# A graph layer with indirect gathers: shorter pauses behind them, an earlier table, and messages in fours across row blocks

## The chip, the cores and the metric

The kernel runs on one core of one Trainium2 chip. The metric is the device time of one execution in microseconds; the profile is of one such execution, and its span runs from the first to the last instruction.

## What is computed

There are N = 2708 nodes with D = 128 features and a dense, mostly zero adjacency matrix `adj` (N x N, rows normalised, with a diagonal). Two layers, each with a residual and a layer norm:

```python
# layer 0: a hyperbolic graph convolution
XW = mobius_matvec(W, X)
gamma = 2.0 / max(1.0 - sum(XW * XW), EPS)
two_mean = (A @ (gamma * XW)) / clamp_abs(A @ (gamma - 1.0))
m = mobius_scalar_mul(0.5, two_mean)
AXW = mobius_scalar_mul(A.sum(-1), m)
x = layernorm(x + expmap0(relu(logmap0(AXW))))
# layer 1: messages over the edges
s = x @ msg_w[:, :D].T ; d = x @ msg_w[:, D:].T
messages = gelu(s[:, None, :] + d[None, :, :] + msg_b)
aggregated = einsum('ijd,ij->id', messages, adj)
h = gelu(concat([x, aggregated]) @ upd_w.T + upd_b) + x
x = layernorm(x + layernorm(h) * ln_w + ln_b)
```

Layer 1 is only worked out for the edges where `adj` isn't zero. All norms of a row (`_norm`, tanh, artanh) are scalars per node.

## The kernel before, in words

The nodes are 22 row blocks of 128. The host only lays the inputs out anew; the kernel does the rest.

**Setup.** `x @ W` and the scalars of every node give `y`, the right side of the first layer's product.

**Layer 0**, a loop over the row blocks. `layer0(b)` loads the block's transposed adjacency `aT` (1408 KB, two buffers), takes its sign on ScalarE (`sgn`, L323) and multiplies by `y` with 22 fp32 products on TensorE (L328). From the signs, `keys` builds numbers that tell where the non-zero columns are (bf16 products, L354, and the eight largest by VectorE, L362), and `extract` turns them into lists of edges in tiles of 128: `J` (column), `rid` (row), `R` (a 0/1 matrix from edge to row), and `F`, the address of the edge's value in `adj` (L452, three buffers). Then GpSimd gathers the values `V` with one indirect DMA per tile of 128 edges. There are 25 lists and 99 tiles (the table `TILES`); `LATE` says how many tiles of a list are reserved for the column blocks from `SPLIT` = 16 on. A block's two steps of `extract` run during the next two blocks.

**Gathers.** All indirect DMAs go through one helper, which puts a pause behind each: a tiny GpSimd instruction of which nothing uses the result.

```python
def gather(o, src, at):
    last = nc.gpsimd.indirect_dma_start(...)
    with tc.issue_after(last.ins):
        nc.gpsimd.tensor_tensor(gap, ones[:, :1], nhalf, op=OP.pow)
```

`issue_after` only orders the pause behind its gather; the scheduler may place it later. The gathers are at L193, the pauses at L197.

**The epilogue of layer 0**, `layer0_end(b0, b1)`, runs on chunks of row blocks, `CHUNKS = [(0, 16), (16, 22)]`: the hyperbolic scalars (L468 to L497, short VectorE instructions on columns of 6 or 16), ReLU and layer norm (L508 to L521), then a transpose (L524), the two products of layer 1 (L532), `s_nm` in SBUF and `dt`, which is written to the DRAM `table` (L539). The first chunk is spread over the blocks after 16, the second comes at the end with high priority.

**Messages.** For each row block, `messages` takes its tiles in fours at most: gather the rows of `table` into `dd` (a ring of 7 buffers of four), spread `s_nm` to the edges with `R` (L690), add (L695), Gelu (L696), and sum to the rows with a matrix `rv` made from the values (L692, L698). `own` adds the node's own edge. For the first 8 row blocks (`EARLY`) the tiles below the split are done first, all after the last epilogue in the program; part of them is gathered into an `aT` buffer. A block's sum then goes through `node`: copy (L660), update product (L609 to L612), Gelu (L613), and in groups of blocks (`GROUPS`) two layer norms (`first`, `finish`, scratch pool `fin` with two buffers) and the output. `step()` advances every waiting `node` by one stage after each call's four.

**Fallback.** At the end flags are summed; if the lists couldn't hold all edges, a dense loop would run. It does not with these inputs.

Each engine executes its instructions in the order of the program as the scheduler has laid it out; the scheduler goes by priorities and by its own estimates of time.

Of the kernel before, what the change touches and what calls it, by code (L numbers as in the profile page):

```python
# [10 lines left out]
F32 = mybir.dt.float32  # L11
U32 = mybir.dt.uint32
# [14 lines left out]
CHUNKS = [(0, 16), (16, 22)]  # L27
GROUPS = [(0, 8), (8, 6), (14, 4), (18, 2), (20, 2)]
EARLY = 8

# [3 lines left out]
SPLIT = 16  # L34
# [3 lines left out]
def group_of(b):  # L38

    if b == 0:  # L40
        return [
            [(0, 1, 8), (1, 2, 8)],
            [(2, 4, 8), (4, 6, 4), (6, 8, 4)],
            [(8, 10, 4), (10, 12, 4), (12, 14, 4), (14, 16, 4)],
            [(16, 19, 4), (19, 22, 4)],
        ]
    s = [4, 2, 2, 1] if b == 1 else [2, 1, 1, 1] if b < 9 else [1] * 4
    return [[(0, 4, s[0]), (4, 8, s[1]), (8, 16, s[2]), (16, 22, s[3])]]
# [5 lines left out]
LATE = [0, 0, 0, 3, 2, 3, 2, 2, 1, 1, 2, 2, 2, 1, 1, 2, 1, 1, 2, 1, 2, 2, 2, 1, 1]  # L54
# [21 lines left out]
def hyperbolic_then_message_kernel(  # L76
# [64 lines left out]
    nc.gpsimd.tensor_scalar(place, place, SPAN, float(SPLIT * P), op0=OP.mult, op1=OP.add)  # L141
# [3 lines left out]
    for i in range(2):  # L145
# [4 lines left out]

    key = const.tile([P, SPLIT], I32, name="key")
    nc.gpsimd.iota(key, pattern=[[-1, SPLIT]], base=127 + 23, channel_multiplier=0)
    nc.vector.tensor_scalar(key, key, 23, None, op0=OP.logical_shift_left)
    kd = const.tile([P, SPLIT, P], BF16, name="kd")
    nc.gpsimd.affine_select(
        kd,
        key.bitcast(F32).unsqueeze(2).to_broadcast([P, SPLIT, P]),
        pattern=[[0, SPLIT], [-1, P]],
# [31 lines left out]
    gap = const.tile([P, 1], F32, name="gap")  # L190

    def gather(o, src, at):
        last = nc.gpsimd.indirect_dma_start(  # L193
            out=o, out_offset=None, in_=src, in_offset=bass.IndirectOffsetOnAxis(ap=at, axis=0)
        )
        with tc.issue_after(last.ins):
            nc.gpsimd.tensor_tensor(gap, ones[:, :1], nhalf, op=OP.pow)  # L197
# [18 lines left out]
    def cols(n):  # L216
        count[0] += 1
        return sc.tile([P, n], F32, name=f"c{count[0]}")

    def rsqrt(v, n, pool=None):  # L220

        if pool is None:
            h, t, o = cols(n).bitcast(I32), cols(n), cols(n)
        else:
            h = pool.tile([P, n], I32, name="rh")
            t = pool.tile([P, n], F32, name="rt")
            o = pool.tile([P, n], F32, name="ro")
# [41 lines left out]
    fin = ctx.enter_context(tc.tile_pool(name="fin", bufs=2))  # L269
# [46 lines left out]
    ss, ssp = cols(NB), cols(NB)  # L316

    def layer0(b):
# [3 lines left out]
        sgn = stream.tile([P, NB, P], BF16, name="sgn", bufs=1)  # L322
        nc.scalar.activation(sgn, aT, AF.Sign, accum_out=signs[:, b : b + 1])  # L323
        op = bank("mp")
        for j in range(NB):
            if j in BREAKS:
                yield
            nc.tensor.matmul(  # L328
                op[:, : D + 2], lhsT=aT[:, j, :], rhs=y[:, j, :], start=(j == 0), stop=(j == NB - 1)
            )  # L330

# [7 lines left out]
            t, v, 0.0, v, op0=OP.max, op1=OP.mult, accum_out=ssp[:, b : b + 1]  # L339
# [3 lines left out]
    def keys(l, sgn):  # L343
# [7 lines left out]
        for i, (j0, j1, _) in enumerate(groups):  # L351
            for j in range(j0, j1):
                q = j if j0 < SPLIT else j - SPLIT + 10
# [16 lines left out]
    def extract(l):  # L370
# [4 lines left out]
        def tmp(name, dt=F32, w=CMAX):  # L375
            return small.tile([P, w], dt, name=name)[:, :C]
# [50 lines left out]
        for k, s in parts:  # L427
            nc.vector.tensor_tensor_scan(scan[:, s], m[:, s], m[:, s], oe[:, l, k : k + 1], op0=OP.add, op1=OP.max)
            nc.vector.scalar_tensor_tensor(
                code[:, s], bits[:, s], 17281.0 + 768 * k, low[:, s], op0=OP.subtract, op1=OP.add  # L430
# [3 lines left out]
        F = small.tile([P, TMAX], U32, name="F", bufs=3)  # L434
# [23 lines left out]
    x1, x1T = x_sb, xT  # L458
    s_nm = mx

    def layer0_end(b0, b1):

        n = b1 - b0
        sb = slice(b0, b1)

        den, r = nom[:, sb, D], nom[:, sb, D + 1]
        di, t, v, e, f = (cols(n) for _ in range(5))
        nc.vector.tensor_scalar_max(di, den, DEN_EPS)  # L468
        nc.vector.tensor_scalar_min(t, den, -DEN_EPS)
        nc.vector.scalar_tensor_tensor(di, den, 0.0, di, op0=OP.is_ge, op1=OP.mult)  # L470
        nc.vector.scalar_tensor_tensor(t, den, 0.0, t, op0=OP.is_lt, op1=OP.mult)
        nc.vector.tensor_add(di, di, t)
        nc.vector.reciprocal(di, di)
        nc.vector.tensor_mul(v, di, di)
        nc.vector.tensor_mul(v, v, ss[:, sb])
        tn, tq = root(v, n)


        a = artanh(tn, n)
        touch(AF.Gelu, a)  # L480
        nc.vector.scalar_tensor_tensor(e, a, 0.5, r, op0=OP.mult, op1=OP.mult)
        nc.vector.tensor_scalar(e, e, FAR, -FAR, op0=OP.min, op1=OP.max)
        nc.vector.tensor_mul(e, e, tq)
        nc.vector.tensor_mul(e, e, di)

        w, p = cols(n), cols(n)
        nc.vector.tensor_sub(w, ss[:, sb], ssp[:, sb])
        nc.vector.scalar_tensor_tensor(p, e, 0.0, ssp[:, sb], op0=OP.is_ge, op1=OP.mult)
        nc.vector.tensor_scalar(t, e, 0.0, None, op0=OP.is_lt)
        nc.vector.scalar_tensor_tensor(w, w, 0.0, t, op0=OP.max, op1=OP.mult)  # L490
        nc.vector.tensor_add(w, w, p)
        nc.vector.tensor_mul(t, e, e)
        nc.vector.tensor_mul(w, w, t)
        un, uq = root(w, n)
        nc.scalar.activation(f, un, AF.Tanh)
        nc.vector.tensor_mul(f, f, uq)
        nc.vector.tensor_mul(f, f, e)  # L497
        if b1 < NB:
            touch(AF.Ln, un)

# [16 lines left out]
        for g, gn in parts:  # L517
# [9 lines left out]
            for k0 in range(0, gn, 2):  # L527
# [8 lines left out]
                last["ACT"] = nc.scalar.copy(dt[:, k0 : k0 + n2, :], sd[:, 1])  # L536
# [5 lines left out]
            last["DVE"] = nc.vector.tensor_add(nom[:, g : g + gn, :D], s_nm[:, g : g + gn, :], dt[:, :gn, :])  # L542

    last = {}
    ends, found, placed = [], [], []
    with tc.issue_after(setup.ins):
        for b in range(NB):
            work = layer0(b)
            next(work)
            for x in placed:  # L550
                next(x, None)
            placed = []
            next(work)
            for x in found:
                next(x)
            placed, found = found, []
            sgn = next(work)
            for l in of_block[b]:
                keys(l, sgn)
                found.append(extract(l))  # L560
            if b == 0 or b == NB - 1:
                for x in found:
                    next(x)
                    next(x, None)
                for x in placed:
                    next(x, None)
                found, placed = [], []
            for e in ends:
                next(e, None)
            for b0, b1 in CHUNKS:  # L570
                if b == b1 - 1 and b1 < NB:
                    ends.append(layer0_end(b0, b1))
                    next(ends[-1])
    for e in ends:
        for _ in e:
            pass
    with tc.high_priority():
        for _ in layer0_end(*CHUNKS[-1]):
            pass
# [3 lines left out]
    gd = nom  # L583
    for ins in last.values():
        ctx.enter_context(tc.issue_after(ins.ins))
    for g, n in quads:
        nc.scalar.activation(gd[:, g : g + n, :D], gd[:, g : g + n, :D], AF.Gelu)
        for k in range(n):
            nc.scalar.mul(gd[:, g + k, :D], gd[:, g + k, :D], dg[:, g + k : g + k + 1])
    xlb = y  # L590
    for g, n in quads:
        nc.vector.tensor_add(xlb[:, g : g + n, :D], x1[:, g : g + n, :], wide(rowvec["lb"], n))
# [64 lines left out]
    def node(h, k, b, b0, n, ag, more, pool):  # L657

        agT = edge.tile([P, P], F32, name="agT")
        nc.scalar.copy(agT, ag[:, :P])  # L660
# [16 lines left out]
    def ring(w):  # L677
        return edge.tile([P, 4, P], F32, name="dd", bufs=RING)[:, :w, :]

    def messages(b, ag, tiles, first, final, bins, room=ring):  # L680

        for q, k0 in enumerate(range(0, len(tiles), 4)):
            ts = tiles[k0 : k0 + 4]
            w = len(ts)
            dd = room(w)
            X = bank(bins[q % len(bins)]).rearrange("p (t d) -> p t d", d=D)[:, :w, :]
            rv = edge.tile([P, 4, P], F32, name="rv", bufs=3)
            for k, t in enumerate(ts):
                gather(dd[:, k, :], table[: SPLIT * P] if t in soon else table, J[:, t : t + 1])
                nc.tensor.matmul(X[:, k, :], lhsT=R[:, t, :], rhs=s_nm[:, b, :], start=True, stop=True)  # L690

                nc.vector.tensor_scalar(  # L692
                    rv[:, k, :], iotaN, rid[:, t : t + 1], V[:, t : t + 1], op0=OP.is_equal, op1=OP.mult
                )
            nc.vector.tensor_tensor(dd, X, dd, op=OP.add)  # L695
            nc.scalar.activation(dd, dd, AF.Gelu)  # L696
            for k in range(w):
                nc.tensor.matmul(  # L698
                    ag[:, :P],
                    lhsT=dd[:, k, :],  # L700
                    rhs=rv[:, k, :],
                    start=(first and k0 == 0 and k == 0),
                    stop=(final and k0 + k == len(tiles) - 1),
                )
            step()

    def own(b, ag):
        nc.tensor.matmul(ag[:, :P], lhsT=gd[:, b, :D], rhs=ident, start=True, stop=False)

# [7 lines left out]
    slab, quads_in = stream.tile([P, NB, P], F32, name="aT"), [0, 0]  # L717

    def roomy(w):
        quads_in[0] += 1  # L720
# [178 lines left out]
```

## Time and profile before

The time is 460.92 us, the median of three runs (460.42 to 465.71). The profiled execution took 460.36 us, its span is 458.6 us, and TensorE was granted 0.791 of its clock on average.

| engine | busy us | share of the span | instructions |
|---|---|---|---|
| TensorE, products | 327.1 | 71% | 2427 |
| TensorE, weight loads | 294.5 | 64% | 2427 |
| VectorE | 281.8 | 61% | 1517 |
| ScalarE | 198.9 | 43% | 538 |
| GpSimd | 331.3 | 72% | 495 |

No engine is busy throughout, so the shares alone don't tell what sets the end. The kernel has stages: setup to about 31 us, layer 0 to about 236, the last epilogue to about 289, messages to about 436, and the last nodes and outputs. The shares have to be read stage by stage, and the busy time of GpSimd counts the issue of a gather and the pause, not the idle time between them. The tile names of the code (`V`, `dd`, `aT`, `gap`, `F`) are the names in the profile's rows.

### The profile page before, as it was taken

Reading aid. Unit: us, or ns where it says so; the run is one execution under the profiler, and the core shown is the slowest. Engines: PE = TensorE matmul, PEld = TensorE weight load, DVE = VectorE, ACT = ScalarE, POOL = GpSimd, SP = SyncE. Lnnn points to the kernel's source line nnn. Section 1 sums busy time; section 2 is a strip of 40 time slices with the busy share of each in tenths; the row PEclk is TensorE's granted clock in tenths of the full one; section 3 lists DMA queues with packets and bytes.
Section 4 is the critical chain, followed back from the end, with each engine's and each line's share of the span. In section 5 each row is a group of like instructions: output and inputs, shape, how many; then the busy total and the mean of one; then the engine's idle time right before and its main releaser. Section 6 shows DMA issues by size and latency. Waiting matters only on the chain.

```text
span 458.6 us, 8002 instructions
## 1 busy us (share of the span) xinstructions
PE 327.1 (71%) x2427; PEld 294.5 (64%) x2427; DVE 281.8 (61%) x1517; ACT 198.9 (43%) x538; POOL 331.3 (72%) x495
## 2 busy tenths in 40 slices
PE   3359999948989999979971007693179777888820
PEld 3249999947989999977871005683168676777710
DVE  1997888832757577997765633992035434445872
ACT  2925676641747675983852303831012111124240
POOL 5400788898898898855278788998888888888200
PEclk9759999987899999998995557798556867575555
DMA  8504543523335464632501112110011111113011
GB/s 324 233 2 151 200 156 128 168 87 126 129 128 206 176 209 174 224 109 85 180 19 30 51 35 69 35 35 1 28 36 35 38 38 34 41 35 83 16 42 39
DMA packets 16238, 45.14 MB, mean 98 GB/s; under 512 B 5626, under 2 KB 11150, under 8 KB 13374
## 3 DMA queue, kind: packets, MB, share of 16 engines
q1 hardware_dynamic: 9710, 37.43, 22.6%
q0 software_dynamic: 6336, 6.55, 6.1%
q10 hardware_dynamic: 144, 0.60, 0.4%
q8 instruction: 20, 0.33, 0.3%
q14 instruction: 28, 0.23, 0.2%
HBM read 41.74 MB, written 2.83 MB: 97 GB/s over the span
## 4 chain that ended last, share of the span: by engine, by line
POOL 36%; PE 29%; DVE 15%; issue 8%; DMA 7%; ACT 3%; POOLq 0%; DVEq 0%
POOL gap L197 14%; PE mp L328 9%; POOL V L193 9%; POOL dd L193 9%; POOL aT L193 4%; DMA dd<-table_dram,J 4%; PE mp L698 4%; PE sel L442 3%; PE X L690 2%; DMA V<-in_adj_dram,F 2%; PE kx L354 2%; PE X L532 2%; PE sel L612 2%; DVE top L362 1%; DMA xT<-in_x_t_dram 1%
## 5 line engine op out<-in xcount | busy, mean ns | idle before, releaser
L193 POOL DMA_INDIRECT V<-in_adj_dram,F x99 | 99.4, 1004 | 57.4 <-DVE top L362 31.0
L328 PE MATMUL mp<-y,aT 128*128 128x130 f32 x968 | 125.8, 285 | 0.9 <-DVE y L312 0.9
L197 POOL TENSOR_TENSOR gap<-ones,nhalf 128x1 f32<-128x1 f32 x198 | 120.7, 610 | 7.1
L328 PEld LDWEIGHTS mp<-y,aT 128*128 128x128 f32 x968 | 118.0, 197 | 1.4 <-DVE y L312 1.1
L193 POOL DMA_INDIRECT dd<-table_dram,J x81 | 79.8, 985 | 25.2 <-issue 13.4
L323 ACT ACTIVATE sgn<-aT 128x2816 bf16<-128x2816 f32 x22 | 56.0, 2545 | 3.9 <-ACT junk L336 3.5
L690 PE MATMUL X<-mx,R 128*128 128x128 f32 x198 | 39.3, 343 | 25.1 <-DVE dd L695 23.5
L695 DVE TENSOR_TENSOR dd<-X,dd 128x384 f32<-128x384 f32 (+3 forms) x29 | 15.1, 526 | 63.8 <-DMA dd<-table_dram,J 60.2
L690 PEld LDWEIGHTS X<-mx,R 128*128 128x128 f32 x198 | 34.2, 250 | 27.7 <-DVE dd L695 24.6
L442 PE MATMUL sel<-z,R 128*128 128x49 f32 (+4 forms) x198 | 30.0, 288 | 22.1 <-DVE R L418 7.3
L442 PEld LDWEIGHTS sel<-z,R 128*128 128x128 f32 x198 | 26.3, 200 | 25.1 <-DVE R L418 8.3
L354 PEld LDWEIGHTS <-sgn 128*128 128x128 bf16 x484 | 29.7, 102 | 18.2 <-issue 9.6
L354 PE MATMUL kx<-kd,sgn 128*128 128x128 bf16 x484 | 35.2, 227 | 7.5 <-ACT sgn L323 7.5
L698 PE MATMUL mp<-rv,dd 128*128 128x128 f32 x116 | 29.1, 414 | 16.0 <-ACT dd L696 13.1
L696 ACT ACTIVATE dd<-dd 128x384 f32<-128x384 f32 (+3 forms) x29 | 13.9, 497 | 55.6 <-DVE dd L695 54.8
L698 PEld LDWEIGHTS mp<-rv,dd 128*128 128x128 f32 x116 | 24.5, 304 | 18.9 <-ACT dd L696 15.1
L413 ACT ACTIVATE work<-iota,mid 128x512 f32<-128x512 f32 (+3 forms) x53 | 26.8, 553 | 22.6 <-DVE mid L406 18.3
L692 DVE TENSOR_SCALAR rv<-iotaN,rid,V 128x128 f32<-128x128 f32 x99 | 30.8, 351 | 3.8 <-PE mp L698 2.9
L362 DVE MAX8 top<-kx 128x8 f32<-128x128 f32 (+3 forms) x152 | 28.5, 234 | 3.7 <-remote 1.6
L524 PE MATMUL kx<-ident,x_sb 128*128 128x128 f32 x22 | 5.8, 356 | 21.7 <-DVE x_sb L521 21.4
L452 DVE SCALAR_TENSOR_TENSOR F<-J,rid 128x3 uint32<-128x3 uint32 (+5 forms) x29 | 4.8, 165 | 26.8 <-DMA V<-in_adj_dram,F 18.7
L366 ACT ACTIVATE junk_s<-kx 128x512 bf16<-128x512 f32 (+2 forms) x25 | 14.1, 563 | 15.6 <-DVE top L362 15.4
(205 smaller groups left out, 611.5 us busy)
## 6 DMA issues: line engine op xcount, KB each, us to landing
aT<-in_adj_t_dram SPq DMA_DIRECT2D x22, 1408.0 KB
V<-in_adj_dram,F POOLq DMA_INDIRECT x99
xT<-in_x_t_dram SPq DMA_DIRECT2D x2, 704.0 KB
x_sb<-in_x_nm_dram SPq DMA_DIRECT2D x2, 704.0 KB
out_dram<-nom SPq DMA_DIRECT2D x21, 64.0 KB
dd<-table_dram,J POOLq DMA_INDIRECT x81
table_dram<-dt SPq DMA_DIRECT2D x5, 256.0 KB
pk<-in_pack_dram ACTq DMA_DIRECT2D x1, 587.5 KB
```

Source lines behind the costliest of these rows:

```text
L193: last = nc.gpsimd.indirect_dma_start(out=o, out_offset=None, in_=src, in_offset=bass.IndirectOffsetOnAxis(ap=at, axis=0))
L197: nc.gpsimd.tensor_tensor(gap, ones[:, :1], nhalf, op=OP.pow)
L323: nc.scalar.activation(sgn, aT, AF.Sign, accum_out=signs[:, b : b + 1])
L328: nc.tensor.matmul(op[:, : D + 2], lhsT=aT[:, j, :], rhs=y[:, j, :], start=(j == 0), stop=(j == NB - 1))
L354: nc.tensor.matmul(kp[:, i * P : (i + 1) * P], lhsT=sgn[:, j, :], rhs=kd[:, q, :], start=False, stop=(i == len(groups) - 1 and j == j1 - 1),)
L362: nc.vector.max(top[:, c : c + 8], seg[:, s, :])
L413: nc.scalar.activation(r0, iota[:, k0 * P : k1 * P], AF.Abs, scale=2.0, bias=mid[:, k : k + 1])
L442: nc.tensor.matmul(sp[:, k, :], lhsT=R[:, t0 + k0 + k, :], rhs=z, start=True, stop=True)
L690: nc.tensor.matmul(X[:, k, :], lhsT=R[:, t, :], rhs=s_nm[:, b, :], start=True, stop=True)
L692: nc.vector.tensor_scalar(rv[:, k, :], iotaN, rid[:, t : t + 1], V[:, t : t + 1], op0=OP.is_equal, op1=OP.mult)
L695: nc.vector.tensor_tensor(dd, X, dd, op=OP.add)
L698: nc.tensor.matmul(ag[:, :P], lhsT=dd[:, k, :], rhs=rv[:, k, :], start=(first and k0 == 0 and k == 0), stop=(final and k0 + k == len(tiles ...
```

## The change

It has these parts, in the order of the diff:

- The pause becomes the sum of two 128 x 128 tiles in place of a power of one column, and it gets high priority, so that the scheduler places it right behind its gather.
- The table is split at row block 13 in place of 16, and the lists' segments follow (`group_of`, `LATE`). `BITS` = 16 keeps the number of bit positions of the keys as before.
- The epilogue runs in three chunks. Its steps are released from within the blocks, by `PARTS`: none, one, two, two steps at successive half blocks. Its scalar part is rewritten: the two square roots go through one chain on a tile of twice the width, and the sign is carried apart.
- `F` has twelve buffers for three, `sgn` two for one, `mp` three for two, the scratch `fin` four for two; `rv` has two for three.
- The row gathers are taken out of `messages` into `fetch`. From row block 14 on (`FETCH`) a call of `fetch` follows each block, so that up to 7 fours of row gathers (the ring) stand among the value gathers of layer 0. The early messages are computed from the end of layer 0 on, between the steps of the last epilogue.
- The tiles of all row blocks form one sequence, cut into fours across the borders of blocks: 25 fours. Up to three sums are open at once. `own` is made when a block's sum opens.

Its core:

```diff
-CHUNKS = [(0, 16), (16, 22)]
+CHUNKS = [(0, 13), (13, 18), (18, 22)]
+PARTS = (0, 1, 2, 2)
+FETCH = 14
-SPLIT = 16
+SPLIT, BITS = 13, 16
...
-    gap = const.tile([P, 1], F32, name="gap")
+    gap = const.tile([P, P], F32, name="gap")
...
-        with tc.issue_after(last.ins):
-            nc.gpsimd.tensor_tensor(gap, ones[:, :1], nhalf, op=OP.pow)
+        with tc.issue_after(last.ins), tc.high_priority():
+            nc.gpsimd.tensor_add(gap, ones, ones)
...
-    fin = ctx.enter_context(tc.tile_pool(name="fin", bufs=2))
+    fin = ctx.enter_context(tc.tile_pool(name="fin", bufs=4))
...
-        sgn = stream.tile([P, NB, P], BF16, name="sgn", bufs=1)
+        sgn = stream.tile([P, NB, P], BF16, name="sgn")
...
-        op = bank("mp")
+        op = bank("mp", 3)
...
-        F = small.tile([P, TMAX], U32, name="F", bufs=3)
+        F = small.tile([P, TMAX], U32, name="F", bufs=12)
...
-        tn, tq = root(v, n)
...
-        un, uq = root(w, n)
+        a = sc.tile([P, 2, NB], F32, name="norms")[:, :, :n]
+        nc.vector.tensor_scalar_max(a, both[:, :, sb], MIN_NORM * MIN_NORM)
+        q = rsqrt(a, n, two=True)
...
+    work = fours([(b, early[b]) for b in range(EARLY)], True)
+    ahead = len(work)
+    work += fours([(b, late[b] if b < EARLY else early[b] + late[b]) for b in range(NB)], False)
...
+    def fetch():
+        if len(rooms) < (len(work) if whole else ahead):
+            dd = edge.tile([P, 4, P], F32, name="dd", bufs=RING)
+            for k, (_, t, *_) in enumerate(work[len(rooms)]):
+                gather(dd[:, k, :], table[: SPLIT * P] if t in soon else table, J[:, t : t + 1])
+            rooms.append(dd)
...
+            if b >= FETCH:
+                fetch()
...
+    for _ in layer0_end(*CHUNKS[-1]):
+        with tc.issue_after(products[-1].ins):
+            for _ in range(2):
+                messages()
```

In the order in which the scheduler lays the changed program out, GpSimd issues 77 value gathers, then 28 row gathers mixed with the value gathers of the last row blocks, then the other 71 row gathers. Nearly every gather has its pause directly behind it; five pauses stand in one row at one place.

## Prediction

> **What bounds the kernel now.** I read the chain that ended last first, then the costliest groups. GpSimd leads the chain, with the gathers and the pauses as its largest lines:
>
> ```profile
> POOL 36%; PE 29%; DVE 15%; issue 8%; DMA 7%; ACT 3%; POOLq 0%; DVEq 0%
> ...
> L193 POOL DMA_INDIRECT V<-in_adj_dram,F x99 | 99.4, 1004 | 57.4 <-DVE top L362 31.0
> ...
> L197 POOL TENSOR_TENSOR gap<-ones,nhalf 128x1 f32<-128x1 f32 x198 | 120.7, 610 | 7.1
> ...
> L193 POOL DMA_INDIRECT dd<-table_dram,J x81 | 79.8, 985 | 25.2 <-issue 13.4
> ```
>
> With the 18 row gathers into `aT` (18.8 us) GpSimd issues 198 gathers of about 1 us and 198 pauses of 0.61 us. Next, its instructions in order of time (start, us):
>
> ```profile
> 238.10 0.95 POOL L193 DMA_INDIRECT dd<-table_dram,J  x1 [0.30 <-issue]
> 239.36 0.95 POOL L193 DMA_INDIRECT dd<-table_dram,J  x1 [0.30 <-issue]
> ...
> 308.08 15.09 POOL L197 TENSOR_TENSOR gap<-ones,nhalf 128x1 f32<-128x1 f32 x24
> 323.42 1.00 POOL L193 DMA_INDIRECT dd<-table_dram,J  x1 [0.25 <-issue]
> 324.45 0.59 POOL L197 TENSOR_TENSOR gap<-ones,nhalf 128x1 f32<-128x1 f32 x1
> 325.21 0.99 POOL L193 DMA_INDIRECT dd<-table_dram,J  x1 [0.17 <-issue]
> ```
>
> A gather with its pause takes 325.21 - 323.42 = 1.79 us, one without 1.25. The first gather starts at 47.5 and the last ends at 427.1: 379.6 us, of which 198 x 1.78 = 352 are this cadence. Real holes are only about 19 us, all between 199 and 230; the largest is the wait for the table. The 24 pauses that the scheduler left behind at 236 to 272 are paid at 308 in one piece. After 427.1 there are 31.5 us of tail. The waits add one more thing:
>
> ```profile
> DVE F L452 <- DMA V<-in_adj_dram,F: 18.7, 8, 7.9
> ...
> POOL dd L193 <- DMA table_dram<-dt: 8.9, 1, 8.9
> ```
>
> `F` has three buffers, so VectorE's lists stand still until gathers have landed. The stretches show what that costs TensorE (columns: PE, PEld, DVE, ACT, POOL busy, clock, DMA share, GB/s):
>
> ```profile
> 90.00:140.00 50.00, 39.34 (x343) 36.48 (x341) 23.12 (x131) 21.74 (x53) 44.83 (x56) 0.86 0.35 122
> 140.00:190.00 50.00, 49.82 (x496) 47.45 (x496) 37.16 (x240) 35.63 (x79) 44.51 (x55) 1.00 0.56 198
> ...
> 236.00:289.00 53.00, 13.85 (x72) 9.65 (x71) 26.84 (x150) 13.63 (x41) 43.46 (x51) 0.63 0.16 44
> ...
> 340.00:390.00 50.00, 40.74 (x202) 35.97 (x202) 22.61 (x94) 10.36 (x32) 44.30 (x57) 0.70 0.15 37
> ```
>
> Layer 0 (31 to 236) is nearly TensorE's, except 90 to 140. From 236 to 289 TensorE starves behind the last epilogue while GpSimd goes on. From 289 GpSimd sets the pace again. So the end is gathers x cadence + holes + tail.
>
> **What the Trainium skill says.** "GPSIMD Engine Reference", section Elementwise, puts a two-input sum at about 2.6 cycles an element (4497 ns for 2048 fp32). No sum runs on this GpSimd, so no trace of before agrees or disagrees; I use it below. "SBUF — State Buffer", section Who interferes with whom, says that a VectorE instruction with two SBUF inputs and a GpSimd instruction that reads SBUF lock each other out. Something like it is visible: among gathers without pauses VectorE's short dependent instructions wait over a microsecond each,
>
> ```profile
> 264.14 0.18 DVE L512 BATCH_NORM_AGGREGATE mv<-st 128x2 f32<-128x6 f32 x1 [1.06 <-DVE st L511]
> 265.55 0.18 DVE L512 BATCH_NORM_AGGREGATE mv<-st 128x2 f32<-128x6 f32 x1 [1.22 <-DVE mv L512]
> ```
>
> where the trace can't say whether the reading or the writing of the gathers is at fault, but which suggests what the pauses are for: to let VectorE through. "Perfetto Trace Analysis", section DMA Instruction — SWDGE (GPSIMD), says a gather's bar ends with its descriptors, not its data; the trace agrees: a bar of 1.0 us, then waits of 2.5 to 3.4 us for `dd` in the chain.
>
> **The change, part by part.**
>
> *The pause.* 198 `pow` on 128x1 become 198 sums on 128x128, each kept behind its gather. Cadence without the pause itself: 1.78 - 0.58 (median) = 1.20 us. Lower bound of the sum: 0.30 us, the one-input tensor_scalar 128x128 at L136. Upper bound: the fixed 0.19 us of a 128x1 tensor_scalar plus 128 x 2.54 ns, the slope of the slowest elementwise row here (128x1024 in 2.79 us), 0.52; with lockouts by a busy VectorE perhaps 0.6. I take fixed 0.19 + 128 x 2.1 ns (the page's slope, an estimate) = 0.46, and add 0.02 for lockouts: cadence 1.68.
>
> *What fills the holes.* The table's first 13 blocks are written inside layer 0, so 28 row gathers (a ring of 7 fours) go in between the value gathers. In the changed program's order 77 value gathers come first, then row gathers and values in turn, 121 in all. When does the first row gather start? By count, 47.5 + 77 x 1.68 = 177. Two waits are later. SyncE holds the table's writes behind the load of block 17's `aT`, which needs block 15 done: at 176 before, minus about 14 of the stall at 90 to 140, plus the first chunk's transposes and products (13 blocks x (0.36 + 2 x 0.46) = 17 us of TensorE) = 179. Four writes through one `dt` buffer, some 2 to 3 us each, partly in flight: 187. The lists of block 14, read two blocks after its end, give 180 to 185. I take 187, so a hole of 10. Then nothing stops GpSimd: the full table is needed at the 37th row gather, 187 + 58 x 1.68 = 284, and the last epilogue should end near 262. GpSimd ends at 187 + 121 x 1.68 = 390.
>
> *F in twelve buffers, `sgn` and `mp` deeper.* Removes VectorE's 18.7 us of waiting; layer 0 ends near 224. Off the path: GpSimd is then behind. Its worth is in the 187 above.
>
> *The epilogue.* 63 short VectorE instructions per chunk become 45: 126 to 135 in all, at 0.17 us + 1.5 us, beside TensorE. The exposed last chunk has 4 blocks for 6 and saves 18 x 0.17 = 3 us. Hidden by the gathers that run on.
>
> *Fours across blocks.* 35 calls become 25, ten fewer sums and Gelus (0.53 + 0.50 us) off the path. They wait for 4 gathers, 6.7 us; TensorE per four needs about 126 us (its busy time after 236) / 25 = 5.0 us, so it keeps up. In the tail three updates instead of one follow the last four's products: 2 x 2.1 us (L609, L611, L612 at 1.83 per block, a Gelu at 0.27) = +4.2; `fin` in four buffers takes away the 2.9 us wait of the reciprocal roots for L643: -2.9. Tail 31.5 + 1.3 = 33.
>
> *Split 13, wider lists, BITS:* the same 4 segments a block; two mixed lists cost a few us of VectorE, hidden by TensorE.
>
> Sum: 390 + 33 = 423, plus 460.4 - 458.6 = 2 between span and device time: 425.
>
> **The rivals.**
>
> *A, the sum is short* (0.30 to 0.36, cadence 1.55): 187 + 121 x 1.55 + 35 = 410. For it: L136. Against: two inputs.
>
> *B, the sum is no shorter than the `pow`* (cadence 1.78): 187 + 215 + 35 = 437. For it: the fixed part of a `pow` may be that of any tensor_tensor (697 ns at 128x2, 582 at 128x1, so 467 fixed). Against: the same rows fit a slow `pow`.
>
> *C, a new wait at the chain of messages:* nothing beside the last epilogue (262), then each four serially: X 1.6, sum 0.5, Gelu 0.5, products 1.6, update 1.6, own product 0.5 = 6.3 us from the rows; 262 + 25 x 6.3 + 35 = 455, no measurable change. For it: TensorE's granted clock is only 0.6 to 0.7 there, and each engine keeps its order. Against: TensorE was at most 0.8 busy, and the ring is seven deep.
>
> *D, slower:* a sum that reads and writes 128 columns is locked out by VectorE, busy 61%, and takes 0.85 us: cadence 2.05, 47.5 + 198 x 2.05 + 35 = 488. For it: the lockout rule. Against: the `pow` averages only 0.03 over its median.
>
> **Chances.** Forecast 0.58, A 0.17, B 0.17, C 0.05, D 0.03. Predicted 425. The range takes in half of A's and nearly all of B's spread, 404 to 446. Faster by over 2% (under 451.7) is forecast, A and B: 0.92; within 2% 0.05; slower 0.03.
>
> **What would show it.** Right: a sum of 0.42 to 0.52 us; cadence near 1.68; row gathers before 200; no hole of GpSimd over 15 us after 50; its last gather near 390; no block of orphan pauses above 5. Wrong: GpSimd idle for tens of us after 190 (then a ring or the table is the bound), VectorE waits for itself of a microsecond during layer 0, or a tail above 45 us.

## The result, and the profile after

The changed kernel takes **425.6 us** (median of 4, 425.2 to 427.2), the kernel before 460.7 on the same occasion: a ratio of **0.923 (0.917 to 0.930)**. 425 was predicted. The sum is right; two of its terms are not, and their errors are opposite and nearly equal.

The page of the changed kernel, chain of waits and costliest groups (after the bar: busy us in all, mean ns of one; then idle us of the engine before them):

```profile
PE 36%; DVE 25%; POOL 12%; ACT 10%; DMA 7%; issue 4%; SPq 2%; DVEq 0%; another core or an unknown queue 0%; POOLq 0%; ACTq 0%
...
L196 POOL DMA_INDIRECT V<-in_adj_dram,F x99 | 97.8, 988 | 59.6 <-DVE bits L433 29.9
...
L196 POOL DMA_INDIRECT dd<-table_dram,J x99 | 97.4, 984 | 32.5 <-DMA table_dram<-dt 17.0
L200 POOL TENSOR_TENSOR gap<-ones 128x128 f32<-128x128 f32 x198 | 83.9, 424 | 4.0
```

GpSimd's share of the chain fell from 36% to 12%, and TensorE and VectorE took its place. That says who was last at each step, not that GpSimd is off the path. Followed back from the end, the chain leaves GpSimd at 285.4 us, at a gather that needs a buffer of the ring which TensorE has just freed (GpSimd had then stood for 0.16 us, as ahead of other gathers), and before that it runs mostly over TensorE and VectorE. So the two are level there, and the chain can't say which of them sets the end; the runs with other pauses can. GpSimd's instructions in order of time show where it stands and where it runs on (start, us, what, and in brackets the idle time before it):

```profile
173.03 0.97 POOL L196 DMA_INDIRECT V<-in_adj_dram,F  x1 [13.52 <-DVE mv L518]
...
199.95 0.95 POOL L196 DMA_INDIRECT dd<-table_dram,J  x1 [16.96 <-DMA table_dram<-dt]
...
300.90 0.97 POOL L196 DMA_INDIRECT dd<-table_dram,J  x1 [0.16 <-issue]
301.89 0.41 POOL L200 TENSOR_TENSOR gap<-ones 128x128 f32<-128x128 f32 x1
302.46 0.97 POOL L196 DMA_INDIRECT dd<-table_dram,J  x1 [0.16 <-issue]
...
390.57 1.05 POOL L196 DMA_INDIRECT dd<-table_dram,J  x1 [0.16 <-issue]
```

The sum takes 0.41 us, and a gather with its pause 302.46 - 300.90 = 1.56 (1.79 before). GpSimd has two holes, 13.5 us for a list that VectorE finishes only between pieces of the epilogue, and 17.0 us for the table. The first row gather starts at 199.95, and the last gather ends at 391.6; in between 120 gathers run without a hole, at 191.7 / 120 = 1.60 (the five pauses left behind included). The tail is 423.4 - 391.6 = 31.8.

The stretches, in the columns of the prediction, show TensorE fed where it starved before: from 39.3 to 47.7 busy us in 90 to 140, from 13.9 to 32.5 in 236 to 289.

```profile
90.00:140.00 50.00, 47.67 (x455) 44.71 (x455) 35.69 (x180) 30.88 (x73) 44.49 (x63) 0.97 0.43 151
...
236.00:289.00 53.00, 32.45 (x232) 29.26 (x229) 41.65 (x204) 22.69 (x64) 46.73 (x68) 0.81 0.11 29
...
340.00:390.00 50.00, 40.30 (x219) 35.89 (x218) 28.77 (x125) 9.76 (x29) 44.39 (x64) 0.73 0.17 43
```

The wait of `F` for gathers is gone from VectorE's waits, but VectorE's busy time rose from 281.8 to 302.9 us. That is the first sign of the term that was missed.

### The profile page after: what moved, and what is told of

Same layout as the page of the kernel before. It is cut to its first block, busy times and chain, and to the rows that moved or that the text cites. A ratio compares the mean times of both kernels' runs of the same rounds, so it can differ in the third digit from the quotient of the medians.

```text
span 423.4 us, 7970 instructions
## 1 busy us (share of the span) xinstructions
PE 318.6 (75%) x2427; PEld 289.3 (68%) x2427; DVE 302.9 (72%) x1524; ACT 200.2 (47%) x538; POOL 292.1 (69%) x495
## 4 chain that ended last, share of the span: by engine, by line
PE 36%; DVE 25%; POOL 12%; ACT 10%; DMA 7%; issue 4%; SPq 2%; DVEq 0%; another core or an unknown queue 0%; POOLq 0%; ACTq 0%
PE mp L337 10%; POOL dd L196 8%; PE kx L364 4%; PE sel L452 4%; PE mp L702 4%; POOL gap L200 4%; DMA aT<-in_adj_t_dram 3%; DMA dd<-table_dram,J 3%; PE X L538 3%; ACT sgn L332 3%; PE X L687 3%; SPq L330 2%; DVE rv L689 2%; DVE R L428 2%; PE kx L285 2%
## 5 line engine op out<-in xcount | busy, mean ns | idle before, releaser
L196 POOL DMA_INDIRECT dd<-table_dram,J x99 | 97.4, 984 | 32.5 <-DMA table_dram<-dt 17.0
L200 POOL TENSOR_TENSOR gap<-ones 128x128 f32<-128x128 f32 x198 | 83.9, 424 | 4.0
L693 ACT ACTIVATE dd<-dd 128x512 f32<-128x512 f32 (+1 forms) x25 | 15.5, 624 | 55.5 <-DVE dd L692 48.5
L452 PE MATMUL sel<-z,R 128*128 128x41 f32 (+5 forms) x198 | 30.6, 287 | 13.8 <-DVE R L428 5.0
L423 ACT ACTIVATE work<-iota,mid 128x256 f32<-128x256 f32 (+3 forms) x54 | 27.6, 560 | 8.3 <-DVE mid L416 6.3
L692 DVE TENSOR_TENSOR dd<-X,dd 128x512 f32<-128x512 f32 (+1 forms) x17 | 11.5, 679 | 20.1 <-DMA dd<-table_dram,J 17.1
L687 PE MATMUL X<-mx,R 128*128 128x128 f32 x134 | 24.4, 322 | 0.0
L687 PEld LDWEIGHTS X<-mx,R 128*128 128x128 f32 x134 | 20.4, 224 | 1.7 <-issue 1.1
L649 PE MATMUL mp<-ident,nom 128*128 128x128 f32 x44 | 10.1, 331 | 12.1 <-ACT nom L706 9.9
L376 ACT ACTIVATE junk_s<-kx 128x384 bf16<-128x384 f32 (+2 forms) x25 | 12.1, 485 | 10.8 <-DVE top L372 6.5
```

The lines of the kernel that those rows point to most:

```text
L196: last = nc.gpsimd.indirect_dma_start(out=o, out_offset=None, in_=src, in_offset=bass.IndirectOffsetOnAxis(ap=at, axis=0))
L200: nc.gpsimd.tensor_add(gap, ones, ones)
L423: nc.scalar.activation(r0, iota[:, k0 * P : k1 * P], AF.Abs, scale=2.0, bias=mid[:, k : k + 1])
L452: nc.tensor.matmul(sp[:, k, :], lhsT=R[:, t0 + k0 + k, :], rhs=z, start=True, stop=True)
```

## The experiments

The theory, T: the end is the time of the first row gather, plus the gathers from there on times their cadence, plus a tail of 32 to 34. Its rivals differ in what else decides; their letters are those of the expectations below, not those of the prediction. The kernels ran in four batches, each on a chip of its own, beside the kernel before (461.4, 461.6, 461.9 and 461.4 us on chips 1 to 4, numbered in the order of the batches); that turned out to matter. None of the batches has the changed kernel itself, and the chip of the result is not on record: a comparison with the changed kernel's trace is one across occasions, unless two runs of one chip are named. Of the gathers from the first row gather on there are 120 in the changed kernel and 108 in the kernel before, counted in the traces; the expectations and the prediction have 121 and 111.

### The pause's length and width

**The old pause in the changed kernel** (ratio to before 0.961, 0.953 to 0.969):

```
-            nc.gpsimd.tensor_add(gap, ones, ones)
+            nc.gpsimd.tensor_tensor(gap[:, :1], ones[:, :1], nhalf, op=OP.pow)
```

> The changed kernel with the pause of before in place of the sum: a pow on 128x1 (0.58 us for 0.41), kept behind its gather. Theory T (GpSimd sets the end from the first row gather on: 200 + 121 gathers x cadence + 32 of tail + 2): the cadence goes back to 1.78, the first row gather stays at 200 because the table, not the count of gathers, releases it; 200 + 215 + 32 + 2 = 449, 23 more than the changed kernel. Rival P (after the table the chain of messages on TensorE and VectorE is the bound, GpSimd only looks busy): less than 12 more, 438 at most. Rival C (the count of gathers also sets when row gathers start): 198 x 0.22 = 44 more, 469.

Measured 444.4 us. The cadence did go back: from the first row gather at 192.7 to the end of the last at 412.0 are 219.3 us, 1.83 each. But that first row gather came 7 us *earlier* than with the shorter sum, and layer 0 ended at 228 in place of 239. A shorter pause should not make layer 0 slower: it points to a second effect of the sum, of the other sign.

**The new pause alone in the kernel before**, with its high priority (0.932, 0.924 to 0.940); a scratch tile of the dense fallback lies in `R` as in the changed kernel, to make room for the wider `gap`, and a few gathers change places:

```
-    gap = const.tile([P, 1], F32, name="gap")
+    gap = const.tile([P, P], F32, name="gap")
...
-        with tc.issue_after(last.ins):
-            nc.gpsimd.tensor_tensor(gap, ones[:, :1], nhalf, op=OP.pow)
+        with tc.issue_after(last.ins), tc.high_priority():
+            nc.gpsimd.tensor_add(gap, ones, ones)
```

> The kernel before with the new pause alone (sum on 128x128, bound to its gather; a scratch tile of the dense fallback lies elsewhere to make room for it). Theory T: its row gathers start at 230 as before, and 111 gathers with pauses follow to 427; at 1.555 for 1.78 they take 25 less, and 460.7 becomes 436, so that the pause alone is 25 of the 35 us of the change. Rival P: in the kernel before TensorE does 112 us of work after 289, where GpSimd would leave it 113 in place of 138; at the 0.8 busy of 340 to 390 it can't, and the time stays above 446. Under rival C the gathers before 230 bring something too: below 425.

Measured 431.2, 30 us less than before. The row gathers start at 224.7, 5 us earlier, and 108 gathers take 173.5 us (1.61 each, 1.82 before). So **the pause alone brings 30 of the 35 us, and everything else in the change 5.6 on top of it**; with the old pause everything else brings 17 (461.4 to 444.4). Rival P falls: TensorE's work after the last epilogue did not hold the kernel before above 446.

**Half the columns** (0.868, 0.860 to 0.875):

```
-            nc.gpsimd.tensor_add(gap, ones, ones)
+            nc.gpsimd.tensor_add(gap[:, :64], ones[:, :64], ones[:, :64])
```

> The changed kernel with the sum on 128x64 in place of 128x128. The sum should take about 0.30 (a fixed 0.19 us of a 128x1 row and half of the other 0.22), the cadence 1.445. Theory T: 200 + 121 x 1.445 + 34 = 409, 17 less with the table as late as now; about 13 if part of the pause is not shortened. Rival P, or rival V (a shorter pause holds VectorE up): less than 5 less than the changed kernel, or more time than it.

Measured 400.2, more than T promised. The sum takes 0.30 us as expected; the cadence is 178.5 / 120 = 1.49, and that makes 13 us of the 25. The other 13 are the first row gather, at 186.9 in place of 200. Again the table comes earlier with a narrower pause.

**Two sums of one column**, to keep the length and take away the width (0.879, 0.873 to 0.886):

```
-            nc.gpsimd.tensor_add(gap, ones, ones)
+            for k in range(2):
+                nc.gpsimd.tensor_add(gap[:, k : k + 1], ones[:, :1], ones[:, :1])
```

> The changed kernel with two sums on 128x1 in place of the one on 128x128, so that the pause stays about as long (0.2 us each, from 0.42 at 128 columns and 0.32 at 64) and touches 2 columns in place of 128. Theory L (the wide sum slows VectorE's instructions on SBUF while it runs, and so layer 0 and the first epilogue; a row of 128x512 took 617 ns with it, 494 with the pow and 486 without pauses): the 128x512 row goes back to about 490, the first table write from 184 to 170 to 177, the first row gather from 200 to 187 to 193, and the whole takes 187 + 121 x 1.58 + 34 = 412. Rival D (the gathers that are held back by the pause are what makes the table late): table and row gathers stay where they are, 425 or more.

Measured 407.0. Two sums take 2 x 0.20 us, the cadence is 186.7 / 120 = 1.56, hardly another than with the wide sum, yet the kernel is 18.6 us faster. The queue of SyncE says why. First the changed kernel's table writes (start, us until the last of them is issued), then those of this one:

```profile
183.61 6.97 SPq L545 DMA_DIRECT2D table_dram<-dt  x3
...
193.40 0.33 SPq L545 DMA_DIRECT2D table_dram<-dt  x1
```

```profile
171.09 6.99 SPq L546 DMA_DIRECT2D table_dram<-dt  x3
...
180.88 0.33 SPq L546 DMA_DIRECT2D table_dram<-dt  x1
```

The first epilogue is 12.5 us earlier, and the first row gather starts at 187.4. VectorE's groups by shape from 60 to 160 us, while layer 0 runs, show what the width does. The changed kernel, then the two narrow sums (the mean ns of one stands before the second bar):

```profile
L372 DVE MAX8 top<-kx 128x8 f32<-128x128 f32 x29 | 7.5, 286 | 2.7 <-PE kx L364 2.7
L428 DVE TENSOR_SCALAR R<-work,deg 128x512 f32<-128x512 f32 x10 | 6.2, 617 | 0.1
...
L433 DVE TENSOR_SCALAR bits<-top 128x48 int32<-128x48 int32 x7 | 2.1, 294 | 0.0
...
L397 DVE MAX8 top<-rest 128x8 f32<-128x24 f32 x7 | 1.2, 171 | 0.1
```

```profile
L373 DVE MAX8 top<-kx 128x8 f32<-128x128 f32 x29 | 7.5, 287 | 3.0 <-PE kx L365 3.0
L429 DVE TENSOR_SCALAR R<-work,deg 128x512 f32<-128x512 f32 x12 | 6.1, 506 | 0.1
...
L434 DVE TENSOR_SCALAR bits<-top 128x48 int32<-128x48 int32 x7 | 1.2, 176 | 0.0
...
L398 DVE MAX8 top<-rest 128x8 f32<-128x24 f32 x7 | 1.2, 175 | 0.1
```

The `tensor_scalar` rows take 617 ns for 506 and 294 for 176 beside the wide sum; the two MAX8 rows don't change, whether they read PSUM (`kx`) or SBUF (`rest`). So the kind of instruction matters, not SBUF alone. The means also hide that part of the instructions of a row are as fast as ever, and others are held up by up to about the length of a sum. Two of the first row in the changed kernel (start, us):

```profile
115.42 0.48 DVE L428 TENSOR_SCALAR R<-work,deg 128x512 f32<-128x512 f32 x1
...
125.14 0.85 DVE L428 TENSOR_SCALAR R<-work,deg 128x512 f32<-128x512 f32 x1
```

This is the lock of the Trainium skill, "SBUF — State Buffer", Who interferes with whom, seen from VectorE's side: `tensor_scalar` can run in a mode that takes both of VectorE's port pairs, one of which is GpSimd's, and whoever holds that pair blocks the other for the whole instruction; an instruction with two SBUF inputs meets GpSimd's reads there, one with a single SBUF input and outside that mode does not. The runs agree in the kinds. Before the first table write VectorE executes the same 742 instructions with either pause. On one chip (the second), `tensor_scalar`, `scalar_tensor_tensor`, `tensor_tensor` and the scan take 15.2 us longer in sum beside the wide sum than beside the narrow ones; MAX8, the reductions, the layer norm's statistics and the `tensor_scalar` that also accumulates stay within 0.1 us for each kind. "For the whole instruction" is not what the `pow` shows: at 0.58 us it is the longest of the pauses, and it leaves the two rows at 494 and 188.

What the width costs has to be read on one chip. Chip 2 ran the wide sum, the narrow sums and no pause, the first and last with the table's writes on ScalarE (an edit that comes below, and that leaves VectorE's 742 instructions in the same order):

| chip 2 | VectorE busy before the first table write | first table write |
|---|---|---|
| sum 128, writes on ScalarE | 144.3 | 178.3 |
| two sums of 1 | 130.5 | 171.1 |
| no pause, writes on ScalarE | 129.2 | 170.2 |

So the width makes VectorE busy for 14 us more, and the table 7 to 8 us later; VectorE waits less in exchange. The other 5 us of the 12.5 don't show on one chip: the changed kernel's trace, from the occasion of the result, has VectorE just as busy (143.9) as the first row of this table but idle for 5.7 us longer, most of it in waits that the profile puts down to issue or to an unknown queue, of which the traces of chips 1 and 2 show next to none. (More on such waits under "Without pauses".) Theory L stands, at 7 to 8 us in place of 13, and rival D falls for the sums. For the `pow` D has a point: on chip 1 its table write comes 7.5 us later than without pauses (176.7 for 169.2) though VectorE is no busier (128.9 and 129.4), so it waits more; for what was not followed up. The half sum has its 128x512 row at 495 though its 128x48 row is at 285: means of 11 and 7 instructions, of which a few are held up (the longest take 574 and 498). It keeps VectorE busy for 134.5 us, 5 more than no pause on the same chip, and the table comes only 1.6 us later.

### Without pauses

**The changed kernel without pauses** (0.808, 0.801 to 0.815):

```
-        with tc.issue_after(last.ins), tc.high_priority():
-            nc.gpsimd.tensor_add(gap, ones, ones)
```

> The changed kernel without any pause: gathers back to back at 1.25. Theory T alone: 200 + 121 x 1.25 + 34 = 385. Rival V (the pauses let VectorE through; without them its short dependent instructions wait about a microsecond each, as at 264 us in the trace of before): the lists and the first epilogue stretch, the table comes later than 215, layer 0 ends after 250, and the whole takes 430 to 460; VectorE then shows idle times before its own instructions that it releases itself.

Measured **373.6**. The first table write comes at 169.2, the first row gather at 185.3, the 120 gathers take 152.9 us, 1.27 each, and the tail 33. There is no sign of rival V here: VectorE's waits for itself are 0.8 us in all. T's 385 assumed that the table stays late.

**The kernel before without pauses** (0.822, 0.814 to 0.829):

```
-        with tc.issue_after(last.ins):
-            nc.gpsimd.tensor_tensor(gap, ones[:, :1], nhalf, op=OP.pow)
```

> The kernel before without any pause, all else the same. Theory T (count x cadence from the first row gather): 225 + 111 x 1.25 + 33 + 2 = 399. Rival P (its messages only begin after the last epilogue near 262, and then TensorE has 112 us of work, at 0.9 busy 124): 262 + 124 + 33 = 419. Rival V (the pauses were there to let VectorE through): 445 or more, with VectorE's own waits of a microsecond, as at 264 in its trace, in all of layer 0.

Measured 380.8, 81 us less than with them. All three expectations are too high; T is nearest. Without any pause the rest of the change is worth 7 us (380.8 to 373.6, on two chips), about what it is worth with the sum.

So the pauses seemed only to cost. The next batch, on another chip, told otherwise. Two kernels without pauses were to bring the table earlier. **Epilogues half a block earlier** (1.068, 1.059 to 1.077), and **two small buffers for `dt`** (1.053, 1.043 to 1.064):

```
-PARTS = (0, 1, 2, 2)
+PARTS = (1, 2, 2, 2)
```

> The changed kernel without pauses, and each epilogue started half a block of layer 0 earlier (PARTS 1, 2, 2, 2 for 0, 1, 2, 2). Theory T: against 373.6 for the kernel without pauses, the first row gather moves from 185 to about 181 and the time with it, to 370, if the full table moves too (it is needed 58 gathers, 73 us, after the first row gather, and came at 257, just in time). Rival P: 373 to 375, since the epilogue earlier is layer 0 later.

```
-            dt = edge.tile([P, 4, D], F32, name="dt", bufs=1)
             for k0 in range(0, gn, 2):
                 n2 = min(2, gn - k0)
+                dt = edge.tile([P, 2, D], F32, name="dt", bufs=2)
...
-            nc.sync.dma_start(
-                table[g * P : (g + gn) * P, :].rearrange("(b p) d -> p b d", p=P), dt[:, :gn, :]
-            )
+                nc.sync.dma_start(
+                    table[i.start * P : i.stop * P, :].rearrange("(b p) d -> p b d", p=P), dt[:, :n2, :]
+                )
```

> The changed kernel without pauses, with dt as two buffers of two blocks in place of one of four, each written to the table on its own. Theory T: copies into dt no longer wait for the write of the four before, the three writes of 7 us take about 5, and the table comes 1 to 2 us earlier: 371.5 to 373. Rival P: 373 to 375.

Measured 492.6 and 486.9, some 115 us *more* than without these edits. The loss begins at 48 us, where the first still runs the very instructions of the kernel without pauses: it can hardly be the edit. So it was run once more, unchanged, in a batch of its own:

> The kernel without pauses and with earlier epilogues once more, not a line changed (it took 492.6 where the kernel without pauses took 373.6, and the traces of the two part at 48 us, while both still run the same instructions in the same order). The two ran in different batches on different chips. Theory C (what back-to-back gathers do to the other engines depends on the chip, or on how the program was laid down that time): on a chip like that of the kernel without pauses it takes 368 to 376, with none of the waits of TensorE, VectorE and ScalarE that the profile puts down to issue or to an unknown queue; on one like the last it takes 490 again, which tells nothing new. Theory S (it is this program): 490 wherever it runs.

Measured **376.5** (0.812, 0.804 to 0.820). **The same kernel takes 492.6 us on one chip and 376.5 on another.** TensorE's instructions from 84 us on, first where it took 492.6:

```profile
85.16 0.68 PE L335 MATMUL mp<-y,aT 128*128 128x130 f32 x4
86.72 0.40 PE L335 MATMUL mp<-y,aT 128*128 128x130 f32 x2 [0.88 <-issue]
88.16 0.43 PE L335 MATMUL mp<-y,aT 128*128 128x130 f32 x1 [1.04 <-issue]
89.57 0.38 PE L335 MATMUL mp<-y,aT 128*128 128x130 f32 x1 [0.98 <-issue]
```

then where it took 376.5:

```profile
84.93 0.54 PE L450 MATMUL sel<-z,R 128*128 128x49 f32 x4
85.31 1.12 PE L335 MATMUL mp<-y,aT 128*128 128x130 f32 x8
86.27 0.17 PE L409 MATMUL sel<-db,tri 128*128 128x2 bf16 x1
86.30 0.16 PE L410 MATMUL sel<-db,ones_b 128*128 128x2 bf16 x1
86.32 2.04 PE L335 MATMUL mp<-y,aT 128*128 128x130 f32 x16
```

Among gathers that follow one another at once, TensorE gets one or two products and then stands a microsecond for nothing that the profile can name. The other engines do the same; from VectorE's waits in the execution of the 492.6 (total us, times, longest; "remote" is an unknown queue):

```profile
DVE rv L687 <- remote: 26.0, 4, 10.5
DVE work L453 <- remote: 17.9, 5, 9.2
```

The gathers themselves are as quick there (0.94 us, 1.25 apart). The waits of a microsecond that the prediction showed at 264 to 266 in the kernel before, among gathers without pauses, look like these; in the kernel before with the new pause, on chip 1, most gathers of 230 to 260 also have none behind them, and VectorE waits for itself nowhere there. The traces of both kernels that the prediction and its result go by have waits of TensorE put down to issue, 7.0 and 6.8 us, and those of chips 1, 2 and 4 at most 0.2: so they seem to come from a chip like the third. On chip 3, that of the 492.6 us, the kernel before took 461.9, and the changed kernel with three buffers for `F`, with its sums, 426.3 with 1.9 us of such waits on TensorE and 4.1 on VectorE, where the kernel of 492.6 has 49 and 81. That is what the pauses buy: **without them these kernels took 374 to 381 us on three chips and 487 to 493 on the other; with them each takes about the same wherever it ran.** Why the engines stand there isn't shown, nor whether it is the chip or something else of that occasion: one kernel ran on both sides, in one batch on each.

With this, the early epilogues show no gain (376.5 to 373.6 without them, on chips 4 and 1), and the small `dt` stays open, since it ran only on chip 3.

### The table's wait, and F

**Table writes from ScalarE's queue**, with the sums (0.928, 0.921 to 0.934) and without pauses (0.823, 0.816 to 0.829):

```
-            nc.sync.dma_start(
+            nc.scalar.dma_start(
                 table[g * P : (g + gn) * P, :].rearrange("(b p) d -> p b d", p=P), dt[:, :gn, :]
```

> The changed kernel with the table's writes issued by ScalarE, which has just written what they send, in place of SyncE, where the fourth write lies behind the load of a block of aT and the loads behind the writes (the scheduler shifts other instructions a little with it). Theory T: the 6 us between the fourth write's issue at 193.4 and the first row gather shrink to 2 or 3, the load of aT is no longer held up, row gathers start near 193, and all of it is gained: 418. Rival P: no gain, since TensorE and VectorE have the same work to do: 424 to 427.

> The changed kernel without pauses and with the table's writes issued by ScalarE. Theory T: against the kernel without pauses (373.6, row gathers from 185) the row gathers start near 178 and the time falls by 5 to 7, to 367 or 368; the full table has to come by 178 + 58 x 1.25 = 251 for this, 6 us before it did. Rival P (the last epilogue then sets the end): 371 to 374.

Measured 429.1 and 380.8, 3.5 and 7 us more than with SyncE's writes on other occasions. ScalarE's instructions in the first of them:

```profile
182.12 0.37 ACTq L545 DMA_DIRECT2D table_dram<-dt  x1
...
184.47 2.55 ACT L332 ACTIVATE sgn<-aT 128x2816 bf16<-128x2816 f32 x1
...
187.02 0.62 ACT L542 COPY dt<-X 128x256 f32<-128x256 f32 x2
...
187.68 0.37 ACTq L545 DMA_DIRECT2D table_dram<-dt  x1
...
194.28 0.27 ACT L542 COPY dt<-X 128x128 f32<-128x128 f32 x1 [1.70 <-DMA table_dram<-dt]
...
194.57 0.34 ACTq L545 DMA_DIRECT2D table_dram<-dt  x1
```

The first write is issued at 178.3, 5 us sooner than in the changed kernel's trace; that isn't ScalarE's doing, since VectorE's instruction just ahead of it ends 5 us sooner too (177.9 for 183.2): these are the 5 us between occasions of above. But the four writes take 16 us in place of 10. The scheduler has laid ScalarE's work out anew, with a `sgn` of 2.55 us ahead of the third pair of copies, which stood behind them before; and the last copy has to wait 1.7 us until the third write, issued at 187.7, has left the only `dt`. The row gathers start at 201. So the wait did not go: it moved from a queue to ScalarE's order and to a buffer. (In which shares was not separated.)

**F in three buffers, as before** (0.926, 0.916 to 0.936):

```
-        F = small.tile([P, TMAX], U32, name="F", bufs=12)
+        F = small.tile([P, TMAX], U32, name="F", bufs=3)
```

> The changed kernel with three buffers for F in place of twelve, all else as it is; the order on every engine stays the same. Theory T: VectorE's lists wait for gathers again (18.7 us in the kernel before), TensorE loses some of its 47.7 busy us of 90 to 140, the first table write comes 3 to 8 later than 184, and the first row gather with it: 429 to 434. Rival (VectorE is behind anyway with the wide sum, so that the gathers it waits for have landed): 425 to 427, with less than 5 us of waits of F for V.

Measured 426.3 on chip 3, no difference from 425.6. The waits are there again,

```profile
DVE F L462 <- DMA V<-in_adj_dram,F: 23.7, 4, 11.0
```

but the first table write comes at 180.7, not later, and the row gathers start at 196.5. What does come later is the last table write, at 291 in place of 277, and GpSimd then stands 5.6 us for messages to make room in the ring. That takes back the gain. So the twelve buffers show no gain. (The 5 us between occasions that the table showed are more than these shifts, so an effect of some 3 us either way would not be seen.)

### Together

Us from the traces (the time is the median); us per gather is from the first row gather to the end of the last, divided by the gathers in between. R is the occasion of the result.

| kernel | chip | first table write | first row gather | us per gather | tail | time |
|---|---|---|---|---|---|---|
| before, `pow` | R | 213.1 | 230.1 | 1.82 | 31.5 | 461 |
| before, sum 128 | 1 | 207.6 | 224.7 | 1.61 | 32.8 | 431.2 |
| changed, `pow` | 1 | 176.7 | 192.7 | 1.83 | 31.6 | 444.4 |
| changed, sum 128 | R | 183.6 | 200.0 | 1.60 | 31.8 | 425.6 |
| changed, sum 128, ScalarE's writes | 2 | 178.3 | 201.1 | 1.61 | 32.4 | 429.1 |
| changed, two sums of 1 | 2 | 171.1 | 187.4 | 1.56 | 31.4 | 407.0 |
| changed, sum 64 | 1 | 170.8 | 186.9 | 1.49 | 33.0 | 400.2 |
| changed, no pause | 1 | 169.2 | 185.3 | 1.27 | 33.1 | 373.6 |
| changed, no pause, ScalarE's writes | 2 | 170.2 | 192.5 | 1.27 | 33.1 | 380.8 |

Each time is the first row gather, 108 or 120 times the cadence, the tail, and about 2 us outside the span. That holds by the way in which the cadence is worked out, so it is no test of T; the tests are that the tail stays at 31 to 33 through all of them, and that the cadence follows the pause. Both narrower pauses beat the changed kernel, by 18.6 and 25.4 us, of which some 5 may be the occasion. Neither was tried on chip 3.

## Why the prediction was right

**The sum that sets the end** was right as a form: start of the row gathers, cadence, tail. The cadence follows the pause in every row of the table, and the tail hardly moves. Its terms:

- *The pause.* 0.46 was the estimate, 0.41 the measurement, and of the 0.02 for lockouts of GpSimd 0.01 shows (the mean is 0.424). The sum takes 0.20 us at 1 column, 0.30 at 64 and 0.41 at 128 in the experiments: 1.7 ns a column, not the 2.1 of the estimate. The cadence of 1.68 was 1.60, and the stretch 192 us for 203: 11 us too many. The cadence lies between the forecast and rival A's 1.55.
- *The first row gather.* 187 was the estimate, 200 the measurement: 13 us too few, and the hole was 17 in place of 10. **The step that failed** is "add 0.02 for lockouts": the lock was charged to GpSimd, in rival D as well, and never to VectorE, whose work lies ahead of the table. It makes VectorE busy for 14 us more there, and the table 7 to 8 us later. The other 5 us are VectorE's longer waits on the occasion of the result; their cause stays open. Layer 0's end (239 for 224) and the last table write (277, where 262 was to be the end of the last epilogue) are late in the same way; with two narrow sums they come at 222 and 256.
- With the narrow sums the first row gather comes at 187.4, so without the lock the total of that term was well sized. Its path was not quite: the load of block 17's `aT` is issued at 161 there, and the first write then waits 10 us for the copy into `dt`; only the fourth stands behind a load, that of block 18. A second hole of GpSimd, 13.5 us for a list, was not forecast; it costs nothing, since the table comes later still.
- That the two errors cancel is luck: 390 was forecast for the last gather's end, and 391.6 it is. The predicted time is nearer than its reasons.
- *Full table in time* was right: GpSimd has no hole after the first row gather. *The tail* was 31.8 for 33.
- *F* was to be worth something "in the 187". No worth shows there: with three buffers the row gathers start no later (196.5, on chip 3).
- *Rival C* (messages as the bound) falls: with 1.27 a gather they still keep up. *Rival D* had the lock, and was wrong in who waits: GpSimd's sum is 0.41 us long, not 0.85.
- The signs named beforehand: no hole over 15 us after 50 was wrong (16.96, the table); a sum of 0.42 to 0.52 was at its edge (0.41 by the median, 0.424 by the mean), and a cadence near 1.68 was just missed (1.60); row gathers before 200, the last near 390, and no block of more than five late pauses came true.
- The reading of the waits at 264, that pauses let VectorE through, fits chip 3, and there TensorE and ScalarE too; on chips 1, 2 and 4 VectorE came through without pauses.

## What to carry to other kernels

A filler on GpSimd should be short and touch few columns: one that reads 128 columns of SBUF made the table of this kernel 7 to 8 us later by holding VectorE up, besides its own time, and the same pause from two single columns did not. When a queue's cadence sets the end, price the start of the queue with the neighbours' slowing included, and look at the same instruction's duration before and after for it, instruction by instruction, since a mean hides who was held up. Put the run to compare with on the same chip. And before a protection is taken out because it only seems to cost, run it on more than one chip.

## What was not expected of the hardware

- The same kernel without pauses took 492.6 us on one chip and 376.5 on another, with waits of 1 to 10 us on TensorE, VectorE and ScalarE that the profile puts down to issue or to an unknown queue. The kernel before, with its pauses of 0.58 us, took 461.4 to 461.9 us on the same four chips, and with the sum of 0.41 us a changed kernel took 426.3 on the chip of the 492.6.
- A sum of 128x128 on GpSimd holds up some of VectorE's instructions by up to 0.4 us (128x512 `tensor_scalar`: 0.48 us or 0.85), those of the kinds named above, and leaves others alone on PSUM and SBUF alike (MAX8: 286 and 287 ns, 171 and 175). A `pow` on one column, though longer, holds up next to none.
